# First scan of a Mamba-like layer: convolution on TensorE with diagonals, fewer rows spread by TensorE, and an earlier way out of the last chunk

## Chip, cores and metric

The kernel runs on one core of one Trainium2 chip. The metric is device time in microseconds (us) of one execution, lower is better. The kernel before takes 3999.52 us (median of three runs, 3998.8 to 4003.98).

## What is computed

The input x has 32 sequences of 256 tokens with 256 channels. A conditioned state-space layer runs first, then two layers of local attention with a gated feed-forward, and the result is added to x:

```
xr, gate = split(x @ W_in.T);  xr = xr + t_emb[:, None, :]
xc  = silu(conv over 4 tokens, one filter per channel (xr) + b_conv)
xn  = layernorm(xc)                       # 512 channels
Bm, Cm, dt = split(xn @ W_xproj.T)        # 16 states
Ad  = 1 + tanh(dt @ W_dt.T + b_dt) * 0.01 * A
Bd  = Bm * min(norm(xn), 1)
for t in range(256):
    h = clip(h * Ad[t] + Bd[t] * xn[t], -10, 10);  y[t] = Cm[t] . h
z = (y + D * xn) * silu(gate) @ W_out.T
z = two layers of (windowed attention, gated feed-forward)(z)
out = x + z
```

All arithmetic that matters here is in 32-bit floats.

## The kernel before

**Groups.** The 32 sequences are worked through in four groups of eight. One group's state (8 sequences x 16 states on 128 partitions, 512 channels on the free axis) is one tile h. The scan of a group has 256 steps; each is one custom VectorE instruction, `step` (L665), that adds a row to h and clips it. The steps are cut into 8 chunks of 32. The scan of group g + 1 is woven into the attention and feed-forward of group g. Only the first scan (`alone`, g == 0) has no such company; and the last group's attention has no scan beside it.

**A chunk.** `load_x` and `project` (L407) make the projection of x; `conv_in` (L437, L443) adds the conditioning to get xr and forms the first tap on GpSimd; `conv_taps` (L454) adds the other three taps on VectorE into acc; `conv_th` (L462, ScalarE) and `conv_out` (L467, VectorE) make the silu, xc. `raw_sums` (L476), `norm_turn` (L506), `norm_stats`, `norm_apply`, `norm_affine` (L540, L541 on GpSimd) and `norm_out` give the normalised rows and write them to DRAM as xnd. `length`, `figures`, `figures_out` (L570), `figures_in` and `decays` make the coefficients: beta that scales each row, ct for the read-out, and the clip bounds. All this runs some 40 steps ahead of the chunk that uses it.

**A step's row.** Row t must stand on all 16 states of its sequence. Either a DMA reads it from xnd with repetition (`load_rows`, L637, on the sync queue, six steps ahead, into one of seven xrep buffers), or, in the first scan only, TensorE spreads it (`spread_rows`, L645): a matmul with 32 rows of contraction, two at a time on different row groups, whose result bx lies in PSUM. `by_tensor` says which: t % 4 < 2, so half of the rows. ScalarE scales either kind by beta (`scale_row`, L658), and `step` consumes it.

**Out of a chunk.** `read_out` (L677) multiplies four h at a time with the diagonal ct (four matmuls with 32 output columns each, on different column groups) into y. `gated` (L726), `out_turn` (L732), `out_gate` (L746), `project_y` (L755), `copy_y` (L766) and `put_y` (L775) apply the skip and gate, project back to 256 channels and write ys to DRAM, from where `load_res` (L883) brings it for the attention, whose first work is `project_qkv` (L912).

**Order.** `group_scan` puts every piece on an agenda: `at(s, what, ...)` puts it at slot s, one slot for each step. `scan_to(s)` emits the slots up to s. The tile framework then orders the instructions of each engine by this order and by which are ready in its own plan; the engines work through their lists strictly in order. Buffers, PSUM banks (eight, all of one pool) and semaphore waits are allotted by the framework. The main part at the end loads layer 0's weights during the first scan, emits slots up to S + 18 (S = 256), loads the residual rows and starts the attention; from there the scan of the next group is emitted evenly with the attention's stages, up to slot 2 S + 18.

Of the kernel before, what the change touches and what calls it, by code (L numbers as in the profile page):

```python
# [10 lines left out]
FP = mybir.dt.float32  # L11
BF = mybir.dt.bfloat16
I32 = mybir.dt.int32
AF = mybir.ActivationFunctionType
ALU = mybir.AluOpType
# [4 lines left out]
P = 128  # L20
S = 256
DM = 256
KM = DM // P
DI = 512
NC_ = DI // P
NS = 16
GB = 8
CH = 32
NCH = S // CH
TB = P // GB  # L30
NQ = 4
# [3 lines left out]
XR = 2  # L35
TAPS = 4
# [16 lines left out]
def bc(ap, axis, n):  # L53

    ap = ap.unsqueeze(axis)
    shape = list(ap.shape)
    shape[axis] = n
    return ap.broadcast_to(shape)
# [15 lines left out]
def kernel(  # L74
# [29 lines left out]
    nc = tc.nc  # L104
# [33 lines left out]
    wc_sb = loaded(w_conv, [P, NC_, TAPS], "wc_sb")  # L138
    bconv_sb = loaded(b_conv, [P, NC_], "bconv_sb")
# [5 lines left out]
    ident = const.tile([P, P], FP, tag="ident", name="ident")  # L145
# [17 lines left out]
    for j in range(NJ):  # L163
# [18 lines left out]
        out=mask_t[:, 0:W], in_=mask_t[:, 0:W], compare_op=ALU.is_ge, fill=MASKED_LOW,  # L182
# [3 lines left out]
        out=mask_t[:, W : 2 * W], in_=mask_t[:, W : 2 * W], compare_op=ALU.is_ge,  # L186
# [29 lines left out]
    for i in range(2):  # L216
        t = const.tile([P, NI * (P + GB)], FP, tag=f"ly{i}", name=f"ly{i}")
# [3 lines left out]
    def program(ctx, exact):  # L221
        rpool = ctx.enter_context(tc.tile_pool(name="res", bufs=1, reuse_waits="tile"))
        wpool = ctx.enter_context(tc.tile_pool(name="weights", bufs=1, reuse_waits="tile"))
        sp = ctx.enter_context(tc.tile_pool(name="sp", bufs=1, reuse_waits="tile"))
# [6 lines left out]
        ps_w = ctx.enter_context(tc.tile_pool(name="psw", bufs=8, space=PSUM, reuse_waits="tile"))  # L231

        def bank(pool, tag, name):
            return pool.tile([P, DI], FP, tag=tag, name=name)
# [150 lines left out]
        def group_scan(g):  # L385
# [7 lines left out]
            b0 = g * GB  # L393
            alone = g == 0

            agendas = [{}]
            state = {"p": one}
            ck = [{} for _ in range(NCH)]

            def at(s, what, *args):  # L400
                agendas[-1].setdefault(s, []).append(partial(what, *args))
# [26 lines left out]
            def conv_in(c, ch):  # L428
                if ch == 0:
                    ck[c]["xc"] = sp.tile([P, NC_, GB * CH], FP, tag="xc", name="xc")  # L430
                ps = ck[c].pop(("ps", ch))
                xr = sp.tile([P, GB, TAPS - 1 + CH], FP, tag="xr", name="xr", bufs=2)
                if c == 0:
                    nc.gpsimd.memset(xr[:, :, 0 : TAPS - 1], 0.0)
                else:
                    nc.gpsimd.tensor_copy(xr[:, :, 0 : TAPS - 1], ck[c - 1]["carry"][:, ch])
                nc.vector.tensor_add(  # L437
                    xr[:, :, TAPS - 1 :],
                    ps.rearrange("p (b t) -> p b t", b=GB),
                    bc(cond_sb[:, ch, b0 : b0 + GB], 2, CH),  # L440
                )
                acc = sp.tile([P, GB, CH], FP, tag="acc", name="acc", bufs=2)
                nc.gpsimd.tensor_scalar(  # L443
                    acc, xr[:, :, 0:CH], wc_sb[:, ch, 0:1], bconv_sb[:, ch : ch + 1],
                    ALU.mult, ALU.add,
                )
                if c < NCH - 1:
                    nc.gpsimd.tensor_copy(ck[c]["carry"][:, ch], xr[:, :, CH:])
                ck[c]["xr", ch] = xr, acc

            def conv_taps(c, ch):
                xr, acc = ck[c]["xr", ch]
                for k in range(1, TAPS):
                    nc.vector.scalar_tensor_tensor(  # L454
                        acc, xr[:, :, k : k + CH], wc_sb[:, ch, k : k + 1], acc,
                        ALU.mult, ALU.add,
                    )

            def conv_th(c, ch):
                acc = ck[c]["xr", ch][1]  # L460
                th = sp.tile([P, GB * CH], FP, tag="th", name="th", bufs=2)
                nc.scalar.activation(th, acc.rearrange("p b t -> p (b t)"), AF.Tanh, scale=0.5)  # L462
                ck[c]["th", ch] = th

            def conv_out(c, ch):
                _, acc = ck[c].pop(("xr", ch))
                nc.vector.scalar_tensor_tensor(  # L467
                    ck[c]["xc"][:, ch], ck[c].pop(("th", ch)), 1.0,
                    acc.rearrange("p b t -> p (b t)"), ALU.add, ALU.mult,
                )  # L470


# [156 lines left out]
                return ck[c]["xnd"].rearrange("(b t) d -> b t d", b=GB)  # L629

            def by_tensor(t):
                return alone and t % NQ < XR

            def load_rows(c, t):
                xr = xp.tile([P, DI], FP, tag="xrep", name="xrep")
# [154 lines left out]
                )  # L790
                rep_w.append(t)

            rep_w = []
            at(-1, start)
            if alone:
                at(-30, spread_weights)
                constants(at)
            for c in range(NCH):
                for t in range(CH):
                    at(c * CH + t, step, c, t)  # L800
            for c in range(NCH):
                s0 = c * CH
                for hb in range(CH // TB):
                    s = s0 + hb * TB
                    for i in range(NI):
                        at(s + 4 * i + 5, read_out, c, hb, i)
                    at(s + 21, gated, c, hb)
                    at(s + 25, out_gate, c, hb)
                    at(s + 11, skip, c, hb)
                for ch in range(NC_):  # L810
                    at(s0 - 38 + 2 * ch, conv_in, c, ch)
                    at(s0 - 37 + 2 * ch, conv_taps, c, ch)
                    at(s0 - 36 + 2 * ch, conv_th, c, ch)
                    at(s0 - 35 + 2 * ch, conv_out, c, ch)
                for ch, s in enumerate((13, 16, 17, 18)):
                    at(s0 + s + 2, gate_th, c, ch)
                    at(s0 + s + 4, gate_out, c, ch)
                at(s0 - 25, raw_copy, c)
                at(s0 - 24, raw_turn, c)
                for j in range(NJ):  # L820
                    s = s0 - 26 + 4 * j
                    at(s + 2, norm_stats, c, j)
                    at(s + 4, norm_shift, c, j)
                    at(s + 5, norm_apply, c, j)
                    at(s + 6, norm_affine, c, j)
                    at(s + 9, norm_out, c, j)
                at(s0 - 11, length, c)
                at(s0 - 9, figures, c)
                at(s0 - 7, figures_in, c)
                at(s0 - 6, decay_th, c)  # L830
                at(s0 - 5, decays, c)
                at(s0 - 4, put_c, c, 0)
                at(s0 + 4, put_c, c, 1)
                for d in range(KM):
                    at(s0 + 45 + 2 * d, copy_y, c, d)
                    at(s0 + 46 + 2 * d, put_y, c, d)
            agendas.append({})
            for c in range(NCH):
                s0 = c * CH
                at(s0 - 43, load_x, c)  # L840
                for ch in range(NC_):
                    at(s0 - 40 + 2 * ch, project, c, ch)
                for ch, s in enumerate((13, 16, 17, 18)):
                    at(s0 + s, project, c, NC_ + ch)
                at(s0 - 27, raw_sums, c)
                for j in range(NJ):
                    at(s0 - 26 + 4 * j, norm_turn, c, j)
                at(s0 - 8, figures_out, c)
                for t in range(CH):
                    if not by_tensor(t):  # L850
                        at(s0 + t - 6, load_rows, c, t)
                    if by_tensor(t) and t % XR == 0:
                        at(s0 + t - 4, spread_rows, c, t)
                    at(s0 + t - 1, scale_row, c, t)
                for hb in range(CH // TB):
                    s = s0 + hb * TB
                    at(s - 9 if alone else s + 7, load_skip, c, hb)
                    at(s + 23, out_turn, c)
                for d in range(KM):
                    at(s0 + 43 + 2 * d, project_y, c, d)  # L860

            return agendas

# [40 lines left out]
        WEIGHTS = [("qkv", 2), ("qkv", 0), ("qkv", 1), ("wo", 0)]  # L904
# [67 lines left out]
        if exact:  # L972
# [4 lines left out]
                out=mask[:, 0:W], in_=mask[:, 0:W], compare_op=ALU.is_ge, fill=MASKED,  # L977
# [3 lines left out]
                out=mask[:, W : 2 * W], in_=mask[:, W : 2 * W], compare_op=ALU.is_ge, fill=MASKED,  # L981
# [402 lines left out]
        def scan_to(s):  # L1384
            while done[0] is None or done[0] < s:
                done[0] = next(scan, 1 << 30)


        DRAIN = 18
        for i, (kind, k) in enumerate(WEIGHTS):  # L1390
            scan_to(100 + 8 * i)
            load_weights(0, kind, k)
        scan_to(S + DRAIN)
        for b in range(GB):
            load_res(0, b)
        for w in range(NW):
# [4 lines left out]
        s0 = done[0]  # L1401
# [130 lines left out]
```

## Time and profile before

| what | value |
|---|---|
| median of three runs | 3999.52 us |
| profiled execution, its own time | 3989.48 us |
| its span | 3987.7 us |
| PE / DVE / ACT / POOL busy | 3769.4 / 2638.7 / 2321.3 / 1739.2 us |
| first step of the first scan | 52.8 us |
| first instruction of the second scan's state (start of h, L781) | 452.4 us |
| first qkv projection | 487.5 us |
| data moved by DMA | 353.51 MB, 89 GB/s on average |

PE is TensorE, DVE VectorE, ACT ScalarE, POOL GpSimd, SP the sync engine that issues most DMAs. The profile cuts the span into 40 slices and gives each engine's busy share in tenths; it lists groups of instructions by line and shape, and it answers with timelines of one engine, where neighbouring instructions of one line are merged and "x8" counts records. A 32-bit matmul leaves two records. An arrow ("<-") names what ended an idle time.

### The profile page before, as it was taken

How to read it: one execution, taken by the hardware profiler on the slowest of the kernel's cores; microseconds unless marked ns; L12 is line 12 of the kernel's file. 1: busy time of each engine (PE TensorE's matmuls, PEld its weight loads, DVE VectorE, ACT ScalarE, POOL GpSimd, SP SyncE). 2: the span in 40 equal slices, each digit the busy share in tenths (PEclk: the TensorE clock that was granted, in tenths of full speed). 3: DMA queues.
4: the chain of work that ended last, by engine and by line, in shares of the span. 5: the costliest groups of instructions: out<-in, count | busy, mean ns of one | idle time of the engine just before them, and what ended most of it. 6: DMA issues, size and time to landing. Idle time of an engine off the chain costs nothing.

```text
span 3987.7 us, 57891 instructions
## 1 busy us (share of the span) xinstructions
PE 3769.4 (95%) x20540; PEld 2359.2 (59%) x20540; DVE 2638.7 (66%) x5241; ACT 2321.3 (58%) x3893; POOL 1739.2 (44%) x1784
## 2 busy tenths in 40 slices
PE   7899889999999999999999999999999999999999
PEld 3333345666656666666666666566666666666666
DVE  6888887777766766767676677676677544444443
ACT  3555556666666566566666656556666555555553
POOL 4443364444444444544445444344444343433431
PEclk8999899999999999999999999999999999999999
DMA  5444533333433434233343434323333111000000
GB/s 152 116 119 118 159 111 110 89 107 103 106 98 97 124 109 128 84 93 94 91 112 94 118 106 116 101 83 101 94 101 103 36 36 44 1 17 20 18 14 23
DMA packets 360414, 353.51 MB, mean 89 GB/s; under 512 B 173795, under 2 KB 220212, under 8 KB 359988
## 3 DMA queue, kind: packets, MB, share of 16 engines
q1 hardware_dynamic: 275666, 337.71, 29.4%
q10 hardware_dynamic: 84450, 12.01, 1.9%
q8 instruction: 165, 2.70, 0.3%
q14 instruction: 133, 1.09, 0.1%
HBM read 314.49 MB, written 33.55 MB: 87 GB/s over the span
## 4 chain that ended last, share of the span: by engine, by line
PE 44%; DVE 16%; ACT 13%; DMA 11%; POOL 9%; issue 5%; ACTq 1%; SPq 0%; DVEq 0%; POOLq 0%
DMA xrep<-xnd 10%; PE ps_qkv L912 9%; PE pa L1247 8%; PE po_f L1275 5%; DVE h L665 5%; PE y L677 3%; ACT xrep L658 3%; PE ps_wo L962 3%; PE sc L1118 3%; PE ov L1156 2%; POOL rn L944 2%; ACT L1255 2%; DVE acc L454 2%; PE ps_in L407 2%; ACT L1127 2%
## 5 line engine op out<-in xcount | busy, mean ns | idle before, releaser
L658 ACT ACTIVATE xrep<-xrep,beta 128x512 f32<-128x512 f32 x896 | 631.1, 722 | 692.2 <-DMA xrep<-xnd 532.4
L665 DVE CUSTOM_DVE_ANT_0 h<-h,xrep,lim 128x512 f32<-128x512 f32 x1024 | 918.6, 897 | 52.7 <-PE y L677 12.5
L912 PE MATMUL ps_qkv<-qkv,res 128*128 128x512 f32 x1536 | 718.0, 604 | 34.6 <-ACT qT L956 21.7
L1247 PE MATMUL pa<-hT,w 128*128 128x256 f32 (+1 forms) x3072 | 693.0, 388 | 28.0 <-ACT pT L1127 26.8
L936 POOL TENSOR_TENSOR rot<-rot,swp 128x512 f32<-128x512 f32 x256 | 344.1, 1344 | 766.3 <-DVE swp L933 621.5
L1247 PEld LDWEIGHTS pa<-hT,w 128*128 128x128 f32 (+1 forms) x3072 | 502.4, 179 | 192.1 <-issue 63.3
L1263 DVE SCALAR_TENSOR_TENSOR ag<-pa,b_sb,ag 128x256 f32<-128x256 f32 (+1 forms) x448 | 213.1, 476 | 594.6 <-ACT ag L1255 593.2
L912 PEld LDWEIGHTS ps_qkv<-qkv,res 128*128 128x128 f32 x1536 | 279.2, 192 | 314.6 <-issue 247.4
L944 POOL TENSOR_TENSOR rn<-ss,neg_half 128x8 f32<-128x8 f32 x256 | 444.2, 1735 | 11.5 <-DVE ss L942 1.6
L1275 PE MATMUL po_f<-ag,w 128*128 128x256 f32 (+1 forms) x1536 | 385.4, 392 | 17.9 <-DVE res L1286 9.3
L677 PE MATMUL y<-h,ly 128*32 128x512 f32 x2048 | 369.1, 620 | 20.1 <-DVE h L665 19.5
L1275 PEld LDWEIGHTS po_f<-ag,w 128*128 128x128 f32 (+1 forms) x1536 | 273.9, 189 | 124.3 <-issue 44.4
L407 PE MATMUL ps_in<-xg,w_in_sb 128*128 128x256 f32 x1024 | 285.9, 410 | 18.0 <-DMA xg<-in_xT_dram 10.4
L945 POOL TENSOR_TENSOR rot<-rot,rn 128x512 f32<-128x512 f32 x256 | 287.7, 1124 | 20.0
L1206 POOL TENSOR_TENSOR rstd<-ve,neg_half 128x1 f32<-128x1 f32 x128 | 77.0, 602 | 486.6 <-DVE ve L1204 486.6
L407 PEld LDWEIGHTS ps_in<-xg,w_in_sb 128*128 128x128 f32 x1024 | 190.8, 199 | 145.7 <-issue 62.0
L928 DVE TENSOR_TENSOR rot<-ps_qkv,rc_sb 128x512 f32<-128x512 f32 x256 | 175.6, 686 | 139.0 <-ACT sq L925 137.8
L1127 ACT ACTIVATE pT<-sc 128x512 f32<-128x512 f32 x384 | 208.3, 594 | 94.9 <-PE sc L1118 93.3
L454 DVE SCALAR_TENSOR_TENSOR acc<-xr,wc_sb,acc 128x256 f32<-128x256 f32 x384 | 203.4, 532 | 89.2 <-POOL acc L443 88.1
L1127 ACT ACT_TABLE_LOAD x185 | 237.4, 1283 | 24.5 <-PE sc L1118 21.5
L1255 ACT ACTIVATE ag<-pa,b_sb 128x256 f32<-128x256 f32 x320 | 151.7, 474 | 156.8 <-PE pa L1247 152.4
L1255 ACT ACT_TABLE_LOAD x186 | 238.6, 1283 | 3.3
(149 smaller groups left out, 5765.7 us busy)
## 6 DMA issues: line engine op xcount, KB each, us to landing
xrep<-xnd SPq DMA_DIRECT2D x896, 256.0 KB
xnd<-xn SPq DMA_DIRECT2D x64, 256.0 KB
qkv<-in_wqkv_dram SPq DMA_DIRECT2D x24, 512.0 KB
xd<-xnd SPq DMA_DIRECT2D x192, 64.0 KB
w<-in_w_dram SPq DMA_DIRECT2D x80, 128.0 KB
xg<-in_xT_dram SPq DMA_DIRECT2D x64, 128.0 KB
ys<-yo ACTq DMA_DIRECT2D x64, 128.0 KB
res<-ys SPq DMA_DIRECT2D x32, 256.0 KB
```

Of the source, the lines that this page charges most:

```text
L407: nc.tensor.matmul(ps, w_in_sb[:, k, ch * P : (ch + 1) * P], ck[c]["xg"][:, k], start=(k == 0), stop=(k == KM - 1),)
L658: nc.scalar.activation(bx, ck[c].pop(("bx", t), bx), AF.Copy, scale=ck[c]["beta"][:, t : t + 1])
L665: nc.vector._custom_dve(TENSOR_ADD_SAT, out=h_new, in0=state["h"], in1=bx, s0=ck[c]["lim"][:, 0, t : t + 1], s1=ck[c]["lim"][:, 1, t : t + 1],
L677: nc.tensor.matmul(ck[c]["y", hb][32 * q : 32 * q + 32, :], ly[hb % 2][:, 32 * t : 32 * t + 32], ck[c].pop(("h", hb * TB + t)), start=(i = ...
L912: nc.tensor.matmul(ps, res[b][:, k, t0 : t0 + W], wt["qkv", a][:, k], start=(k == 0), stop=(k == KM - 1),)
L936: nc.gpsimd.tensor_add(rot, rot, swp)
L944: nc.gpsimd.tensor_tensor(rn, ss, neg_half, ALU.pow)
L945: nc.gpsimd.tensor_mul(rot, rot, bc(rn, 2, DH))
L1127: nc.scalar.activation(p, banks[r], AF.Exp)
L1247: nc.tensor.matmul(pg if x else pa, wt["w1", m][:, k, x], self.h[:, k], start=(k == 0), stop=(k == KM - 1),)
L1255: nc.scalar.activation(ag[0:n], pg, AF.Gelu, bias=b1g)
L1275: nc.tensor.matmul(self.po[:, d], wt["w2", 0][r0 : r0 + n, m, d * P : (d + 1) * P], self.ag[m][r0 : r0 + n], start=(m == 0), stop=(m == le ...
```

## The change

In the first scan only:

- **Convolution.** The four taps become matmuls on TensorE: each multiplies xr, shifted by k tokens, with a 128 x 128 diagonal matrix of the channel's tap weights, and a matmul with a contraction of one row adds the bias. They accumulate in PSUM, where ScalarE and VectorE read them. The first tap on GpSimd and the three on VectorE go. The sixteen diagonals (four taps for each of four blocks of channels), the bias row and a row of ones are made once, in the buffers that later hold the qkv weights.
- **Rows.** `by_tensor` becomes t % 8 < 2: a quarter of the rows are spread by TensorE, three quarters come by DMA.
- **Weights.** wo, w1 and w2 are asked for first, from slot 64 on; qkv at slot 226, since its buffers hold the diagonals until the last convolution.
- **Last chunk.** The second half of the first scan's last chunk has its gate, transpose, output projection, copy and store at earlier slots, and the main part goes on at S + 7 in place of S + 18.

```diff
+            def end(c, hb):
+                return alone and c == NCH - 1 and hb == CH // TB - 1
...
             def conv_taps(c, ch):
...
+                    acc = bank(ps_w, "w", "ps_conv")[:, 0 : GB * CH]
+                    nc.tensor.matmul(
+                        acc,
+                        tap_w[2][0:1, 0, ch * P : (ch + 1) * P],
+                        tap_w[2][0:1, 1, 0 : GB * CH],
+                        start=True,
+                        stop=False,
+                    )
+                    for k in range(TAPS):
+                        nc.tensor.matmul(
+                            acc.rearrange("p (b t) -> p b t", b=GB),
+                            tap_w[ch // KM][:, ch % KM, k * P : (k + 1) * P],
+                            xr[:, :, k : k + CH],
+                            start=False,
+                            stop=(k == TAPS - 1),
+                        )
...
             def by_tensor(t):
-                return alone and t % NQ < XR
+                return alone and t % (2 * NQ) < XR
...
+            def tap_weights(i):
+                t = wpool.tile([P, KM, DI], FP, tag=f"qkv{i}", name="tap_w")
+                nc.vector.tensor_mul(
+                    t.rearrange("p c (k n) -> p c k n", k=TAPS),
+                    bc(bc(ident, 1, TAPS), 1, KM),
+                    bc(wc_sb[:, i * KM : (i + 1) * KM], 3, P),
+                )
+                tap_w.append(t)
+
+            def tap_bias():
+                t = wpool.tile([P, KM, DI], FP, tag="qkv2", name="tap_b")
+                nc.scalar.dma_start(
+                    out=t[0:1, 0].rearrange("p (c n) -> p c n", c=NC_),
+                    in_=b_conv.rearrange("p c -> c p").unsqueeze(0),
+                )
+                nc.gpsimd.memset(t[0:1, 1], 1.0)
+                tap_w.append(t)
...
+                for i in range(NC_ // KM):
+                    at(-41, tap_weights, i)
+                at(-41, tap_bias)
...
-                    at(s + 21, gated, c, hb)
-                    at(s + 25, out_gate, c, hb)
+                    at(s + (21, 18)[end(c, hb)], gated, c, hb)
+                    at(s + (25, 19)[end(c, hb)], out_gate, c, hb)
...
-                    at(s0 + 45 + 2 * d, copy_y, c, d)
-                    at(s0 + 46 + 2 * d, put_y, c, d)
+                    at(s0 + (45 + 2 * d, 37 + d)[end(c, 1)], copy_y, c, d)
+                    at(s0 + (46 + 2 * d, 37 + d)[end(c, 1)], put_y, c, d)
...
-                    at(s + 23, out_turn, c)
+                    at(s + (23, 18)[end(c, hb)], out_turn, c)
...
-                    at(s0 + 43 + 2 * d, project_y, c, d)
+                    at(s0 + (43 + 2 * d, 36)[end(c, 1)], project_y, c, d)
...
-        for i, (kind, k) in enumerate(WEIGHTS):
-            scan_to(100 + 8 * i)
+        for i, (kind, k) in enumerate(WEIGHTS[3:] + WEIGHTS[:3]):
+            scan_to(S - 30 if kind == "qkv" else S // 4 + 8 * i)
             load_weights(0, kind, k)
-        scan_to(S + DRAIN)
+        scan_to(S + 7)
```

`bc` broadcasts an operand along a new axis; `bank` takes one PSUM bank.

## The prediction

> **What bounds the kernel now.** I read the forty slices first, then busy time by stage, then the costliest groups and the timelines of TensorE (PE) and VectorE (DVE) in one chunk of the first scan, and last the way out of that scan.
>
> ```profile
> PE   7899889999999999999999999999999999999999
> DVE  6888887777766766767676677676677544444443
> ```
>
> From the sixth slice on PE is at its ceiling and DVE is not. The first five slices (500 us) are the first scan, which no attention accompanies. A kernel that is PE-bound afterwards gains only by ending this scan sooner without leaving PE work for later. The steps of the first scan run from 52.8 to 451.9 us: 399 us for 8 chunks of 32 steps. A table of busy time for a steady chunk (us, PE, weight loads, DVE, ACT, POOL, clock, DMA share, GB/s):
>
> ```profile
> 299.50:349.00 49.50, 45.14 (x172) 17.97 (x169) 45.07 (x83) 29.59 (x55) 19.88 (x26) 0.93 0.42 119
> ```
>
> Both PE and DVE are busy 91% of it, so neither can be the bound alone: each waits for the other in its fixed order. Groups of instructions by shape, 100 to 400 us (about 6 chunks; busy us, mean ns, idle before):
>
> ```profile
> L677 PE MATMUL y<-h,ly 128*32 128x512 f32 x384 | 107.5, 657 | 7.1 <-DVE h L665 6.6
> L645 PE MATMUL bx<-xq,rep_w 32*128 32x512 f32 x194 | 61.1, 638 | 0.0
> L407 PE MATMUL ps_in<-xg,w_in_sb 128*128 128x256 f32 x192 | 57.3, 437 | 0.0
> ...
> L454 DVE SCALAR_TENSOR_TENSOR acc<-xr,wc_sb,acc 128x256 f32<-128x256 f32 x73 | 36.8, 504 | 5.6 <-POOL acc L443 5.6
> ```
>
> A matmul leaves two records here (L407 issues 16 a chunk, and 192 records stand for 6 chunks). How long does one take? The PE timeline says it (start, length, line, count of records):
>
> ```profile
> 250.03 1.07 PE L677 MATMUL y<-h,ly 128*32 128x512 f32 x8
> 251.02 1.13 PE L407 MATMUL ps_in<-xg,w_in_sb 128*128 128x256 f32 x4
> 252.08 1.13 PE L645 MATMUL bx<-xq,rep_w 32*128 32x512 f32 x4
> ...
> 255.53 1.04 PE L677 MATMUL y<-h,ly 128*32 128x512 f32 x2
> ```
>
> From start to start: two full 256-column matmuls 1.06, so 0.53 each; a pair of bx 1.06; four y in a row 1.0, but one y alone also 0.98. And DVE, beside the convolution:
>
> ```profile
> 305.10 0.48 DVE L454 SCALAR_TENSOR_TENSOR acc<-xr,wc_sb,acc 128x256 f32<-128x256 f32 x1 [0.46 <-POOL acc L443]
> 305.50 0.81 DVE L665 CUSTOM_DVE_ANT_0 h<-h,xrep,lim 128x512 f32<-128x512 f32 x1
> 306.23 0.63 DVE L454 SCALAR_TENSOR_TENSOR acc<-xr,wc_sb,acc 128x256 f32<-128x256 f32 x1
> ```
>
> A tap takes 0.40 of DVE from start to start, waits for POOL's first term now and then, and is slower (0.63) while POOL works. The way out, from the last output projection to the first qkv:
>
> ```profile
> 472.77 0.70 PE L755 MATMUL ps_out<-zT,w_out_sb 128*128 128x256 f32 x2
> ...
> 487.48 8.35 PE L912 MATMUL ps_qkv<-qkv,res 128*128 128x512 f32 x12 [6.54 <-ACT xrep L658]
> ```
>
> From the last step at 451.9 to qkv at 487.5 are 35.6 us; the named releaser had long been done, the data came through ys and the res loads (issued from 482.5).
>
> **What the Trainium skill says.** "TensorE: Matmul & The Clock Gate", Part 3 on packing small matmuls: a small contraction or output saves nothing by itself, only neighbours on other row or column groups overlap. The trace agrees: one y 0.98, four 1.0. "Trainium Kernel Development and Optimization", Performance Expectations: matmul busy time is a poor measure of nearness to the limit. Here it holds for y: 18 us busy per chunk (17.36 in the chunk above, mean 18.4), where eight runs of four would need 8. "SBUF — State Buffer", Who interferes with whom: a DVE operation with two SBUF inputs and a POOL operation that reads SBUF exclude each other. The trace agrees in kind: POOL's first term takes 0.56 alone and 1.28 beside DVE. "DMA: Bandwidth & Descriptors", Queues, rings and completion order: descriptors of one issuing engine's ring are consumed in order. No row of before shows a large load in the middle of the first scan.
>
> **The change, part by part.** The order in which the changed program issues its instructions shows that it does what it says: 32 convolutions of 5 matmuls, 64 bx in place of 128, 192 row loads in place of 128, and no L454 in the first scan.
>
> *DVE per chunk.* Out: 12 taps x 0.40 = 4.8, waits for POOL's first term 5.6/6 = 0.9, slowing beside POOL 4 x 0.2 = 0.8. Back: taps filled the gap between dependent steps (0.88 from step to step back to back, 0.72 with something between); the new order has 11 such pairs a chunk, the old 8: 3 x 0.16 = 0.5. Net -6.0 to -6.4. xc now reads PSUM; other DVE rows that read PSUM (L437, 415 ns; L746, 667) are no slower than SBUF ones, so nothing. ACT's th likewise (its PSUM row is 677, its SBUF row 721).
>
> *PE per chunk.* In: 4 x 5 x 0.53 = 10.6, the one-row bias priced as a full matmul (bounds 0 to 0.53; nothing on other row groups is next to it). Out: 4 bx pairs, and the split pairs: nine runs become four, 5 x 1.06 = 5.3. y: the old order has 12 runs a chunk (up to 18 in the first), the new one 8, and the single y that wait for single steps are gone. Sum for a new steady chunk: y 8.0, bx 4.2, ps_in 8.5, conv 10.6, ps_out 3.9, ps_raw 2.0, transposes 3.1, ps_st 1.0 = 41.3. The same sum for the old one is 40 against 45 busy and 49.5 elapsed.
>
> *The new wait.* On PE the convolution waits for xr, which DVE writes (L437), and behind it stand the next ps_in and a run of y. Who waits for those: DVE's next xr, and the h buffers. In the new order each xr stands at least one step ahead of its convolution, so I price no wait beyond the stretches below. PSUM has eight banks; a chunk takes 34 of them in turn now and 30 after the change (8 bx fewer, 4 convolutions more), so none is short.
>
> *Together.* PE and DVE meet every four steps, when a run of y needs its fourth h. In the new order the eight PE stretches are about 6.8, 7.4, 4.7, 4.2, 4.7, 5.1, 4.2, 3.7 us (two convolutions fall into the second, ps_in and bx into the first). Those of DVE, with steps at 0.74 to 0.88 and the waits for POOL's powers (10.3/6 = 1.7) that stay, are 4.9, 4.8, 4.3, 4.1, 4.7, 6.1, 5.5, 6.5. The later of each pair sums to 45.9. Eight h buffers let DVE run ahead of PE in the first two: I take 1 off, 45.0. Bounds: 43 (DVE alone, 49.5 - 6.4) to 48. Gain 4.5 a chunk. The convolutions of chunks 1 to 7 fall into the first seven; chunk 7 carries that of the next group, on DVE as before, and no gain. 7 x 4.5 = 31.5.
>
> *Row loads.* 24 of 32 rows now come by DMA: 8 x 262 KB more, 5.9 to 8.0 MB a chunk, 176 GB/s at 45 us. Between 455 and 487 us, with every row loaded, 24 steps took 33 us (1.4 each) at 191 GB/s. So the rate is there, and I price it at nothing; cover is the seven row buffers. Without it ACT waits for 2 to 4 us more a chunk, as it does now behind xnd. SP issues 8 more at 0.52, 4 us, beside waits of its own.
>
> *Ramp.* The two tap tables (128x1024 products, by L726's 680 ns for 512 about 1.4 each) and the small bias load fall into DVE's 3.8 us idle and before x lands at 10.4. The four convolutions then take PE 10.6 in the ramp, where DVE needed 12 taps; POOL's chain (L289, L540, L541) ends last. 0, bounds -3 to +3.
>
> *Weights.* wo, w1, w2 move ahead, qkv behind: 1.5 MB now stand on SP's queue after row 150 of 192, with row loads behind them. At 260 GB/s, which full windows show, they need 6 us; row buffers hold some 4. Once +2, bounds 0 to 6.
>
> *Way out.* Its last transposes, zT and ps_out now stand directly after the last y, and nothing but 14 steps of the next group stands ahead of qkv. Old steps 1 to 14 of that group end 21 us after the scan; the path y, transpose, ps_out (about 8) plus the old 14.7 from ps_out to qkv gives 23. So 35.6 becomes 23: -12.6. PE work shifted behind it: eight ps_in 4.2, two y, small ones: +5.6. Net -7, bounds -12 to -2. Eleven slots less in the drain mean the second scan's remaining steps are spread 4% denser over a PE-bound stretch; their PE work is the 5.6 already counted.
>
> *Sum.* -31.5 - 7 + 2 = -36.5. The profiled execution took 3989.5 (span 3987.7), so 3953; the median of the runs is 10 higher, 3999.5, so 3963.
>
> **Rivals.** *DVE was the whole bound:* each chunk loses 6.4 and the way out 12.6: 45 + 13 = 58, 3942. For it: DVE's waits on PE inside a chunk are small (h idle 5.4 in 300 us). Against: PE's 7 us stretches. *PE hands the gain back in part:* its 41.3 with all its old idle (4.4) and some 2 of remaining waits, 48 a chunk: 10.5 + 7 - 2 = 15.5, 3984. *Slower:* in the convolution's stretch the y do not close up, because h still arrive singly, each waiting for a row. Then y stay at 18.4 and PE's busy time is 45.1 - 5.3 + 10.6 = 50.4, with 4.4 idle 54.8: +5.3 x 7 = 37, less 5, 4032. It decides from y above about 14 us a chunk. Against it: the order itself writes them in fours.
>
> **Numbers.** Forecast 3963 (3950 to 3977) 55%; DVE the whole bound, 3942, 12%; partly handed back, 3984, 15%; slower, 4032, 15%; anything else 3%. About 0.2%, 8 us, is what a measurement of this kernel can tell from no change. Faster 78%, within it 8% (upper end of the third case, lower of the fourth), slower 14%. The range 3940 to 3988 takes in the first three.
>
> **What would show it.** Right: chunks of about 45 us, PE near 42 busy with y at 9 to 11, DVE near 39; no L443 or L454 before the second scan; qkv some 23 us after the last step. Wrong: y still 15 or more a chunk, ACT's waits for row loads grown past 4 us a chunk, or a gap of over 6 us where qkv is loaded.

## The result, and the profile after

The kernel before took 4003.87 us (median of 13 runs beside those of the changed kernel), the changed one 3990.97 (3981.46 to 3996.99): a ratio of 0.9968 with a 95% interval of 0.9959 to 0.9976, 13 us less where 37 were forecast. The profiled execution of the kernel before was a lucky one, 14 us under that median, and that of the changed kernel 6 under its own; so the two spans, 3987.7 and 3983.4, differ by only 4. Totals below are therefore ratios, each against runs of the kernel before on the same chip; stages are read from the traces.

The slices of the changed kernel, PE and DVE:

```profile
PE   7888789989999999999999999999999999999999
DVE  5878777677777766767676677676667544444443
```

DVE has become lighter in three of the first five slices (the first scan), and PE is no fuller there. Busy time of a steady chunk of the changed kernel (start:end, length, PE, weight loads, DVE, ACT, POOL, clock, DMA share, GB/s):

```profile
196.14:244.07 47.93, 42.19 (x198) 22.60 (x196) 37.42 (x69) 29.36 (x56) 17.06 (x29) 0.96 0.62 167
```

The chunk lost 1.6 us of 49.5, though DVE lost 7.6 of busy time and PE 3. Both now stand idle for longer. Groups of the changed kernel, 100 to 400 us:

```profile
L703 PE MATMUL y<-h,ly 128*32 128x512 f32 x402 | 77.1, 630 | 4.5 <-DVE h L691 4.4
L471 PE MATMUL ps_conv<-xr,tap_w 128*128 128x256 f32 x177 | 44.3, 390 | 0.0
L671 PE MATMUL bx<-xq,rep_w 32*128 32x512 f32 x100 | 31.4, 634 | 0.0
...
L463 PE MATMUL ps_conv<-tap_b 1*128 1x256 f32 x44 | 15.3, 426 | 0.0
```
```profile
L493 DVE SCALAR_TENSOR_TENSOR xc<-th,ps_conv 128x256 f32<-128x256 f32 x23 | 9.7, 421 | 21.4 <-ACT th L489 21.2
...
L552 DVE SCALAR_TENSOR_TENSOR stat<-mv,stat 128x1 f32<-128x1 f32 x12 | 3.0, 250 | 17.9 <-POOL stat L547 17.5
```

```profile
L596 PE MATMUL ps_st<-rhs,sel 128*128 128x96 f32 x24 | 6.6, 417 | 24.3 <-ACT xrep L684 20.5 <-DVE rhs L588 3.8
```

The same three places in the kernel before:

```profile
L467 DVE SCALAR_TENSOR_TENSOR xc<-th,acc 128x256 f32<-128x256 f32 x24 | 11.5, 479 | 4.8 <-ACT th L462 4.8
L526 DVE SCALAR_TENSOR_TENSOR stat<-mv,stat 128x1 f32<-128x1 f32 x12 | 7.2, 598 | 10.3 <-POOL stat L521 10.3
L570 PE MATMUL ps_st<-rhs,sel 128*128 128x96 f32 x24 | 6.3, 402 | 17.5 <-DVE rhs L562 14.6 <-ACT xrep L658 2.9
```

On PE, y fell from 107.5 to 77.1 and bx from 61.1 to 31.4; the convolution came in with 59.6. On DVE the waits for ACT's th (now L493) and for the power on POOL (now L552) rose from 4.8 and 10.3 us to 21.4 and 17.9; PE's wait at ps_st, the product of the figures, rose from 17.5 to 24.3. In one chunk they look like this; first DVE, then POOL, then PE:

```profile
219.67 0.17 DVE L552 SCALAR_TENSOR_TENSOR stat<-mv,stat 128x1 f32<-128x1 f32 x1 [4.26 <-POOL stat L547]
219.79 0.81 DVE L691 CUSTOM_DVE_ANT_0 h<-h,xrep,lim 128x512 f32<-128x512 f32 x1
```
```profile
217.86 1.27 POOL L567 TENSOR_TENSOR xn<-xn,lnb_sb 128x512 f32<-128x512 f32 x1
219.09 0.55 POOL L547 TENSOR_TENSOR stat<-ve,neg_half 128x1 f32<-128x1 f32 x1
```
```profile
232.78 1.14 PE L596 MATMUL ps_st<-rhs,sel 128*128 128x96 f32 x4 [4.21 <-ACT xrep L684]
```

DVE stands 4.26 us at a tiny operation, with steps of h queued behind it. What it waits for is a power on POOL (L547, the inverse root of a variance), and POOL does that only after its passes over xn of the chunk's first half (L566, L567). Some thirteen microseconds on, PE stands 4.21 us at the product of the figures, with the next chunk's ps_in and a run of y behind it. (In the kernel before the second wait was 2.9, the first 1.7.)

The way out, on PE:

```profile
448.11 5.16 PE L781 MATMUL ps_out<-zT,w_out_sb 128*128 128x256 f32 x16 [1.10 <-DVE zT L772]
...
463.08 3.24 PE L961 MATMUL ps_qkv<-qkv,res 128*128 128x512 f32 x7 [0.64 <-DMA res<-ys]
```

From the last step (ends 439.7) to qkv are 23.4 us, as forecast, and qkv starts 24.4 us earlier than before. But from there to the end it takes 3520.3 us in place of 3500.2. Most of the head start is given back. (The profiled execution before was fast for its kernel, so these 20 us are too many rather than too few.)

### The profile page after: what moved, and what is told of

The parts are those of the page before. It is cut to its first block, busy times and chain, and to the rows that moved or that the text cites. A ratio compares the mean times of both kernels' runs of the same rounds, so it can differ in the third digit from the quotient of the medians.

```text
span 3983.4 us, 58306 instructions
## 1 busy us (share of the span) xinstructions
PE 3756.7 (94%) x20732; PEld 2400.9 (60%) x20732; DVE 2586.4 (65%) x5147; ACT 2325.8 (58%) x3893; POOL 1715.3 (43%) x1753
## 4 chain that ended last, share of the span: by engine, by line
PE 44%; DVE 15%; ACT 14%; DMA 11%; POOL 10%; issue 5%; ACTq 1%; SPq 0%; DVEq 0%; POOLq 0%
DMA xrep<-xnd 10%; PE ps_qkv L961 9%; PE pa L1296 8%; PE po_f L1324 5%; DVE h L691 4%; ACT xrep L684 4%; POOL rn L993 3%; PE ps_wo L1011 3%; PE y L703 2%; PE ov L1205 2%; PE sc L1167 2%; ACT L1304 2%; PE ps_in L412 2%; POOL rot L985 2%; DVE acc L480 2%
## 5 line engine op out<-in xcount | busy, mean ns | idle before, releaser
L684 ACT ACTIVATE xrep<-xrep,beta 128x512 f32<-128x512 f32 x960 | 677.2, 722 | 721.9 <-DMA xrep<-xnd 508.8
L691 DVE CUSTOM_DVE_ANT_0 h<-h,xrep,lim 128x512 f32<-128x512 f32 x1024 | 912.6, 891 | 65.8 <-PE y L703 17.9
L703 PE MATMUL y<-h,ly 128*32 128x512 f32 x2048 | 322.7, 617 | 14.5 <-DVE h L691 14.4
L1011 PE MATMUL ps_wo<-oT,wo 128*128 128x256 f32 x1024 | 231.5, 379 | 0.0
```

The lines of the kernel that those rows point to most:

```text
L684: nc.scalar.activation(bx, ck[c].pop(("bx", t), bx), AF.Copy, scale=ck[c]["beta"][:, t : t + 1])
L691: nc.vector._custom_dve(TENSOR_ADD_SAT, out=h_new, in0=state["h"], in1=bx, s0=ck[c]["lim"][:, 0, t : t + 1], s1=ck[c]["lim"][:, 1, t : t + 1],
L703: nc.tensor.matmul(ck[c]["y", hb][32 * q : 32 * q + 32, :], ly[hb % 2][:, 32 * t : 32 * t + 32], ck[c].pop(("h", hb * TB + t)), start=(i = ...
L1011: nc.tensor.matmul(po[:, d], wt["wo", 0][:, c, d * P : (d + 1) * P], oT[:, c, :], start=(c == 0), stop=(c == NC_ - 1),)
```

## The experiments

"Chunk" is the mean interval of 32 steps over chunks 1 to 5, read from the starts of the h steps in each trace; "behind" is the time from the first qkv to the end. Chunk, qkv and behind come from one trace each. The change, e3 and e11 have the same loop and agree in the chunk to 0.1 us, but their first steps come between 53.5 and 58.1 us, so a few microseconds in the last two columns mean nothing. Each expectation says what it means by its theories.

| kernel | ratio to before (95%) | chunk, us | qkv at, us | behind, us |
|---|---|---|---|---|
| before | 1 | 49.7 | 487.5 | 3500.2 |
| the change | 0.9968 (0.9959 to 0.9976) | 48.1 | 463.1 | 3520.3 |
| e3 convolution and rows | 0.9942 (0.9928 to 0.9955) | 48.2 | 479.5 | 3495.3 |
| e1 convolution alone | 0.9995 (0.9983 to 1.0006) | 50.6 | 491.8 | 3494.7 |
| e2 rows alone | 0.9977 (0.9969 to 0.9985) | 48.7 | 482.5 | 3504.6 |
| e4 way out alone | 1.0016 (1.0009 to 1.0022) | 49.5 | 477.0 | 3525.6 |
| e7 change, half the rows | 1.0031 (1.0020 to 1.0043) | 51.1 | 486.1 | 3522.4 |
| e6 change, no bias | 0.9950 (0.9936 to 0.9964) | 47.8 | 457.1 | 3517.1 |
| e10 e3, figures later | 0.9967 (0.9955 to 0.9979) | 48.4 | 489.8 | 3489.9 |
| e14 e3, one power | 1.0030 (1.0019 to 1.0041) | 49.0 | 480.7 | 3521.2 |
| e16 e10, xg by POOL | 1.0014 (1.0005 to 1.0024) | 47.5 | 497.4 | 3497.1 |
| e17 e3, xn by DVE | 0.9898 (0.9884 to 0.9912) | 43.6 | 454.7 | 3500.8 |
| e18 e16 and e17 | 0.9947 (0.9934 to 0.9959) | 46.3 | 483.5 | 3493.7 |
| e21 before, xn by DVE | 0.9967 (0.9956 to 0.9978) | 46.9 | 468.6 | 3502.4 |
| e25 e3, third pass on POOL | 0.9984 (0.9976 to 0.9992) | 49.0 | 488.8 | 3497.8 |
| e26 before, third pass | 1.0035 (1.0025 to 1.0045) | 50.7 | 502.6 | 3500.2 |
| e11 change, scan first | 0.9947 (0.9935 to 0.9959) | 48.2 | 473.5 | 3501.9 |
| e22 change, xn by DVE | 0.9904 (0.9885 to 0.9923) | 43.1 | 437.4 | 3521.3 |

**The parts.** e3 leaves out the short way out, e4 puts it alone on the kernel before (the same slots, and `scan_to(S + 7)`); e1 and e7 keep half the rows on TensorE, e2 changes the rows alone. e3, e1 and e7 keep the changed order of the weights.

```diff
 e3, e1:
-                return alone and c == NCH - 1 and hb == CH // TB - 1
+                return False
-        scan_to(S + 7)
+        scan_to(S + DRAIN)
 e1, e7 (e2 the other way round, on the kernel before):
-                return alone and t % (2 * NQ) < XR
+                return alone and t % NQ < XR
```

> The change without the shorter way out (slots of the last chunk and S + 18 as before); convolution by TensorE, quarter of the rows, order of the weights as changed. Theory P (in the first scan TensorE's own list sets the chunk: 42 us of work and 5.5 us of waits in its order): chunks stay near 47.7 us, the first scan still ends near 440 us, qkv starts some 12 us later than in the changed kernel (475), and from qkv to the end it takes 10 to 15 us less than there (3505 to 3510), because work that the early start pushed behind it is done before; total 3991 to 3997. Rival (the prediction's sum: an earlier start is worth 7 us net): total 7 us above the changed kernel, 3998.

> The kernel before with the shorter way out alone. Theory P with the early start given back: qkv starts 10 to 14 us earlier than before (475), from there to the end it takes nearly as much longer (3508 to 3514 where before took 3500); total within 4 us of before, 4000 to 4004. Rival (the prediction's sum): 7 us less than before, 3997.

> The changed kernel with half of the rows spread by TensorE again. Theory P: four more pairs of bx, 4.2 us more TensorE work a chunk, chunks near 52 us, the first scan some 30 us longer, total 4015 to 4022, slower than before. Rival D (rows that come late by DMA hold the chunk at 47.7): with 8 loads fewer a chunk gets shorter, 45 to 47, total 3975 to 3990. Rival W (VectorE's waits in its own list): chunks unchanged, total 3991.

> The kernel before with one edit: a quarter of the rows spread by TensorE, convolution still on VectorE, way out as before. PE loses some 4.2 us of bx a chunk, VectorE loses nothing. If the gain of the change comes from VectorE's lighter list (theory V), the chunk stays at 49 to 49.5 us and the time at 0.999 to 1.001 of the kernel before. If the gain comes from fewer spread rows alone, and the convolution by TensorE gives nothing or takes back (theory R; the change with half the rows was 1.003), the chunk falls to 46.5 to 47.7 and the ratio to 0.992 to 0.996.

> The change's convolution by TensorE alone: half the rows still spread by TensorE, way out as before. With the short way out this was 1.0031; that way out costs 0.0016 to 0.0026. So 1.0005 to 1.0015 if the parts add. The rows alone gave 0.9977, both together 0.9942: then the two edits are worth more together than their sum (0.998 to 0.999). If it is under 0.998, they simply add and the half rows in the run with the short way out lost elsewhere.

The loop's two edits together gain 0.58%, 23 us (18 to 29). Neither does so alone: the convolution nothing (its chunk is 1 us longer, and the chunk beside the load of qkv takes 56.3), the rows 0.23%. A reading that fits is that PE, busy 46 of 51 us in e1, has no room for 10.2 us of convolution until bx gives some back. e7 bears it out: four more pairs of bx, 4.2 us, made the change's chunk 3.0 us longer. The way out costs 0.16% alone; with the rest it takes 0.26 points off e3's gain. That is the first half of the answer: without its third part the change is faster. Only e7 came out as its theory said; e3 was better and e4 dearer than either of their theories, e1 and e2 lay between theirs.

By its first qkv e3 is only 8 us ahead of the kernel before (479.5 against 487.5), and its steady chunk gains 1.5 us. The other 15 of its 23 us lie behind. Part of that is the fast profiled execution before, which was not fast in the first scan: e4, with the same first scan, ends it at 451.5 us against 452.3. The rest wasn't looked into.

**Is PE's work the bound of the chunk?** e6 leaves out the bias matmul, and so the addition of b_conv: four matmuls of 0.62 us a chunk.

```diff
-                    nc.tensor.matmul(acc, tap_w[2][0:1, 0, ...], tap_w[2][0:1, 1, ...],
-                        start=True, stop=False)
-                            start=False,
+                            start=(k == 0),
```

> The changed kernel without the bias matmul (it leaves out the convolution's bias, and starts the sum with the first tap). Theory P: 4 x 0.62 = 2.5 us less TensorE work a chunk, chunks near 45.3 us, total 14 to 18 us less than the changed kernel, 3973 to 3977. Rivals D and W: chunks unchanged, total within 3 us of 3991.

The first chunk fell to 43.7 us (47.4), steady ones stayed at 47.6 to 48.0. But e6 does not decide. PE's run from ps_st to the transposes is as long as with the bias, 24.4 us, with the same number of y and ps_in in it: they take about 1.4 and 0.8 us longer. In e6's list one of the runs of four y is split into three and one, and what stands behind PE's wait is slowed for longer (1.94 us for four y; the change has 1.40 there):

```profile
181.65 1.94 PE L696 MATMUL y<-h,ly 128*32 128x512 f32 x8
185.28 1.06 PE L696 MATMUL y<-h,ly 128*32 128x512 f32 x6
190.31 1.04 PE L696 MATMUL y<-h,ly 128*32 128x512 f32 x2
```

So PE was spared little, 1.0 us of busy time a chunk, and the chunk fell by 0.4; the total, 7 us under the change, lies between the theories. The chain of e3, in order of time (start, length), suggests another bound, which e17 and e26 below test:

```profile
211.33 0.59 PE tp_x L532 x4
...
219.11 1.28 POOL xn L566
...
220.47 1.27 POOL xn L567
221.73 0.52 POOL stat L547
...
222.28 0.18 DVE stat L552
...
231.54 0.72 ACT sq_x L573 x2
...
235.38 0.71 PE ps_st L596 x2
```

It is a ring. PE works without a stop from ps_st at 187.4 through the next chunk's ps_in and convolutions to the transposes of the norm at 212; then 23 us of latency lead over POOL, DVE, eight steps of h held up at L552, and ACT back to ps_st at 235.4: 25 + 23 = 48. (From sq_x the data of ps_st go over DVE's ss at 232.4, a second power on POOL at 232.7, 1.2 us long, and rhs on DVE at 233.9; the view follows ACT's list, which runs beside them.)

**Where can the ring be shortened?** e10 puts figures_out, figures_in, decay_th, decays and put_c one slot later; e14 does both halves' power in one instruction, with the steps that use it behind; e16 is e10 with xg loaded through GpSimd's list; e17 gives the two passes over xn to VectorE in the first scan; e18 is e16 and e17; e21 is e17's edit on the kernel before. The edits of e10, e14 and e16 hold in all four scans, those of xn in the first alone.

```diff
 e10:
-                at(s0 - 8, figures_out, c)
+                at(s0 - 7, figures_out, c)
 e14:
-                nc.gpsimd.tensor_tensor(stat[:, j, 0:1], ve, neg_half[:, 0:1], ALU.pow)
+                if j == NJ - 1:
+                    nc.gpsimd.tensor_tensor(stat[:, :, 0], ve, neg_half[:, 0:NJ], ALU.pow)
 e16:
-                    nc.sync.dma_start(out=xg[:, k], ...)
+                    nc.gpsimd.dma_start(out=xg[:, k], ...)
 e17, e21:
+                eng = nc.vector if alone else nc.gpsimd
-                nc.gpsimd.tensor_mul(xn, xn, lng_sb)
-                nc.gpsimd.tensor_add(xn, xn, lnb_sb)
+                eng.tensor_mul(xn, xn, lng_sb)
+                eng.tensor_add(xn, xn, lnb_sb)
```

> The change with the long way out (0.9942 of the kernel before), and in it the product of the figures (ps_st on PE) with what follows it (figures_in to put_c) one step later. In the trace of the change PE stands 4.2 us a chunk at ps_st, behind it the y runs, the next chunk's ps_in and its convolution. If that wait sets the chunk (theory L, a chain through lists kept in order), the chunk falls by 2 to 4 us and the ratio to 0.987 to 0.990. If the wait only takes up slack (the chunk is set by VectorE's stall at stat or by the chain of h), the chunk stays at 47 to 48 and the ratio at 0.993 to 0.996; if the later figures make h wait, it is 0.996 or more.

> The change with the long way out (0.9942), and in it one power on GpSimd for both halves of the chunk, with both norm_shifts, norm_applys and xn passes after it, so that the power of half 1 no longer stands behind the two xn passes of half 0. VectorE waits 4.3 us a chunk there (stat behind POOL), with steps of h behind it. If this stall sets the chunk (theory S), the wait goes, the chunk falls by 2 to 4 us and the ratio to 0.987 to 0.990. If the chain over PE's wait at ps_st sets it (theory L), the stall moves: the last xn pass comes no earlier, since both now follow half 1, the wait at ps_st stays at 4 us or grows, and the ratio stays at 0.993 to 0.997.

> The change with the long way out, the product of the figures one step later (alone that gave 0.9967: PE's wait of 4 us went from ps_st to the next chunk's ps_in, which waited for xg behind the writes of xn and the loads of xq in SP's list), and xg loaded through GpSimd's list in place of SP's. Theory R (ring): PE's next run starts when xg is there, and no more at 191.4 us but at 185 to 187 us in the same chunk's time, 1 to 5 us a chunk less than the 48.3 of the figures alone: 44 to 47, ratio 0.987 to 0.993. Theory V: PE's wait goes, or moves to the y runs, and the chunk stays at 47.5 to 48.5, ratio 0.994 to 0.998.

> The two edits of the runs beside it together: figures one step later with xg through GpSimd's list, and xn by VectorE in the first scan. Theory R (ring): both waits leave the ring, so the gains add until VectorE's work (37.5 + 2.5 us) or PE's (42) sets the chunk: 42 to 45, ratio 0.980 to 0.989. Theory V: 47.5 to 50, ratio 0.994 to 1.000.

> The change with the long way out (0.9942 of the kernel before; chunks 47 to 48 us), and in the first scan the two passes over xn (norm_affine) by VectorE in place of GpSimd, so that the power of half 1 has no pass ahead of it on GpSimd and each pass takes less time (1.28 us on GpSimd). Theory R (ring): the steady chunk is a ring of 24.5 us in which PE works through its list from ps_st to the transposes of the norm without a stop, and 23.5 us of latency from these transposes over stat, xn, power, stat, eight steps of h, sq_x, rhs back to ps_st. This edit takes 2.5 to 5 us out of the latency and adds some 2.5 us of work to VectorE, which has 8 to 10 us of slack: chunk 43.5 to 46, ratio 0.984 to 0.991. Theory V (VectorE's work and the chain of h set the chunk, the stalls only take up slack): the chunk stays at 47.5 or grows by up to 2.5 us, ratio 0.994 to 0.999.

> The kernel before (convolution by VectorE) with the one edit that in the first scan VectorE does the two passes over xn in place of GpSimd. In the kernel before VectorE was busy 44 to 45 of 49.4 us. If VectorE's work set the chunk there (the ring is what the change made the bound), 2.5 us more of it cost 1 to 3 us a chunk: ratio 1.001 to 1.005. If the ring over the norm set the chunk there already, it gains as it does with the change: ratio 0.990 to 0.997.

e10 missed: PE's wait went from ps_st to the next ps_in and was about as long (3.5 to 4.1). The PE timeline of e10:

```profile
191.44 2.04 PE L412 MATMUL ps_in<-xg,w_in_sb 128*128 128x256 f32 x4 [3.50 <-DMA xg<-in_xT_dram]
```

The loads of xg stand in SP's list behind the loads of xq, which wait for the written xn; so xg closes the same ring a second time. e16 takes it out of that list, and PE still waits 2.3 to 3.1 us a chunk at ps_in: xg through GpSimd lands late. The view of that tile in e16:

```profile
DMA to landing us min/median/max: 5.8/6.7/7.8
```

(through SP the chain of e10 shows 3.6.) e18 keeps that wait, 2.3 to 4.7, and is worse than e17 alone. e16's steady chunk, 47.5, is even shorter than e3's; it loses at the start (first step at 64.6 us against 56.3, first chunk 53.8 against 47.5). e14 moves the stall from L552 to the steps of h (3.0 to 3.4 us a chunk, e3 1.5 to 1.9), and 26 us of its loss against e3 lie behind the first scan (3521.2 against 3495.3), where the same norm runs beside attention: a wait exchanged for a wait. e14 and e16 came out worse than either of their theories. e17 is the hit, 43.6 us a chunk. Two groups of e17, 100 to 400 us:

```profile
L567 DVE TENSOR_TENSOR xn<-xn,lng_sb 128x512 f32<-128x512 f32 x12 | 8.2, 685 | 1.5 <-ACT xn L559 1.5
...
L552 DVE SCALAR_TENSOR_TENSOR stat<-mv,stat 128x1 f32<-128x1 f32 x14 | 3.8, 273 | 5.4 <-POOL stat L547 5.0
```

A pass takes 0.69 us in place of 1.27, as the Trainium skill has it ("GPSIMD Engine Reference", Engine selection: an elementwise operation with two inputs is about twice as slow on GpSimd). The power no longer queues, and the wait at L552 falls from 19.7 us (e3) to 5.4. PE's wait at ps_st falls from 4.2 to 0.3 in chunks 2 and 3. DVE got 2.7 us more work a chunk and the chunk became 4.7 us shorter. PE's busy time fell by only 0.8 us (42.4 to 41.6), so it was not PE's sum that set the chunk. The same edit gained 2.8 us a chunk in the kernel before.

The edit did more than shorten the latency, though. Here are the steps of h, e3 and then e17:

```profile
L691 DVE CUSTOM_DVE_ANT_0 h<-h,xrep,lim 128x512 f32<-128x512 f32 x196 | 169.6, 865 | 12.6 <-ACT xrep L684 4.7 <-DVE h L691 2.9 <-PE ps_raw L502 0.8
L692 DVE CUSTOM_DVE_ANT_0 h<-h,xrep,lim 128x512 f32<-128x512 f32 x214 | 178.6, 835 | 9.6 <-ACT xrep L685 2.6 <-PE y L704 1.9 <-DVE h L692 1.0
```

With less work on POOL beside it a step takes 0.03 us less, 1 us a chunk; DVE's busy time rose by 0.9 us and not by 2.7, and in e21 it fell, from 44.6 to 43.4. And PE, without its long wait, kept a higher clock, 0.98 over these chunks in place of 0.94 (last section).

Was it the latency, or only less crowding on GpSimd? e25 (on e3) and e26 (on the kernel before) add a pass on GpSimd, and no work to PE or VectorE:

```diff
                 nc.gpsimd.tensor_add(xn, xn, lnb_sb)
+                if alone:
+                    nc.gpsimd.tensor_scalar_mul(xn, xn, 1.0)
```

> The change with the long way out (0.9942), and in the first scan a third pass over each half of xn on GpSimd, a multiplication by 1.0, behind the power of half 1. It adds 1 to 2.5 us of latency a chunk between the norm and the product of the figures, and no work to PE or VectorE; GpSimd is idle 30 us of 48. Theory R (the chunk is a ring through this latency): the chunk grows by 1 to 2.5 us, ratio 0.996 to 0.999. Theory T (moving xn to VectorE helped only by ending the contention of GpSimd's passes with VectorE's, or by the earlier power): 0 to 0.5 us, ratio 0.993 to 0.9955.

> The kernel before with the same third pass on GpSimd in the first scan. Moving xn to VectorE gained 0.9967 there too. If the ring bound the kernel before as well, the chunk grows by 1 to 2.5 us, ratio 1.002 to 1.0045; if it was bound by VectorE's work with the power of half 1 in it, 0 to 0.5 us, ratio 0.9995 to 1.0015.

The pass takes 1.7 us a half and stands behind the power, on an engine that is idle for 30 us of the chunk; 17 us were lost in one kernel and 14 in the other (0.42 and 0.35%). Part of the loss lies in the chunks (0.7 and 1.0 us each, where 1 to 2.5 were expected), part in the start of the scan (in e26 the first chunk takes 59.4 us, before 53.3). In e26 DVE's busy time did not grow (44.6 and 44.3 us a chunk), so there it is latency that made the chunk longer: the ring was in the bound of the kernel before, which the prediction did not have. In e25 DVE's busy time grew by 1.0 us as well, so there latency and crowding are not told apart. How much of e17's 4.7 us is latency, crowding or clock was not separated.

**The way out.** e11 keeps the short way out and the early loads of res, but does the scan's list up to its old point before the first projections.

```diff
             load_res(0, b)
+        scan_to(S + DRAIN)
         for w in range(NW):
```

> The whole change, short way out included, but the last steps of the scan's list (S + 7 to S + 18, which hold early work of the second scan) are put before the first projections of the first sequence and not beside them; only the loads of res stay early. The change itself was 0.9968, with the long way out 0.9942. Theory G (the early start of attention only brings forward work that then shares PE with what the second scan's start needs, and the later sequences give it back): qkv begins near 473 us in place of 463, the part after it falls from 3520 to 3495 to 3500, and the ratio is 0.992 to 0.9945. If instead the shortened steps of the last chunk themselves (gated, out_turn and project_y moved up) cause the loss, the part after stays at 3515 or more and the ratio is 0.996 to 1.0.

> The whole change, short way out and all, with the two passes over xn by VectorE in the first scan. With the long way out this edit gave 0.9898. If the price of the short way out (0.9968 against 0.9942) is paid behind the first scan and has nothing to do with its chunks (theory G), it is paid again: 0.9915 to 0.993, and the second scan's first 32 steps take 88 to 92 us in place of 79. If the price came from the chunks being late, it goes: 0.988 to 0.990.

e11 starts qkv 10 us later than the change, "behind" falls from 3520 to 3502, and the total by 0.21 points, 8 us. So the moved steps of the last chunk are innocent of most of it; the cost is that projections start before the second scan has its early work done. The total, 0.9947, is just above what this theory said (0.992 to 0.9945). In the changed kernel, on DVE:

```profile
483.28 4.40 DVE L691 CUSTOM_DVE_ANT_0 h<-h,xrep,lim 128x512 f32<-128x512 f32 x4
495.06 0.69 DVE L977 TENSOR_TENSOR rot<-ps_qkv,rc_sb 128x512 f32<-128x512 f32 x1 [7.37 <-ACT sq L974]
```

VectorE waits 7.4 us for squares of the projections, and the steps of the second scan stand behind: from its step 14 to 24 it takes 45.7 us (before 24.2), for its first 32 steps 90.6 (before 80.8, e11 75.2, e4 90.9, e22 89.6). PE, which is the bound there, starves a little later. Busy time of 520 to 600 us, first the change, then e11:

```profile
520.00:600.00 80.00, 66.46 (x372) 38.40 (x369) 61.52 (x115) 44.32 (x83) 42.03 (x43) 0.94 0.42 113
```
```profile
520.00:600.00 80.00, 72.54 (x427) 40.11 (x425) 68.13 (x129) 46.78 (x88) 44.88 (x48) 0.98 0.47 129
```

The trace of e22 speaks against a link with the chunks: with them at 43.1 us qkv starts at 437.4, and "behind" is 3521.3 again. Its total does not show it: 0.9904 can't be told from e17's 0.9898, while the price seen between e3 and the change would make it 0.9924, which is just outside its interval (to 0.9923). Which wait accounts for which part of the 20 us was not separated; what PE loses in the first eight sequences, both layers, is 13.7 us of idle and 9.1 of busy time, some of it at a lower clock.

## Why the prediction was wrong

*The direction held, the size did not:* 13 us came of 36.5 in the sum, and 3991 lies above the range. Two steps failed: "Together", which made the loop 6.5 us worse than forecast by the totals, and "Way out", 17 us. None of the three signs named for being wrong appeared; they watched for other failures. Term by term:

- *DVE per chunk, -6.0 to -6.4:* right or a little low; busy 45.1 to 37.4 in the chunks shown.
- *PE's sum, 41.3:* 42.2 busy, right in part by luck. y takes 12.3 us a chunk where 8.0 was summed and 9 to 11 named as the sign of success: single y were not gone. The other terms came out lower (a convolution 2.55 us, four taps 1.93 and the bias 0.62, against 2.65 priced; the transposes 2.5 against 3.1), and the busy time counts overlaps once. The slower rival (y stays at 18) fell.
- *"Together", the later of each pair of stretches, 45.9, less 1:* this step failed. It let PE and DVE wait for each other alone. The waits for POOL's powers "that stay" at 1.7 became 2.9; the waits of xc for ACT's th went from 0.8 to 3.4; and "no wait beyond the stretches" on PE left out ps_st, 4.2 us. All three are places of one ring through PE, ACT, POOL and DVE, whose latency DVE's lighter list hardly shortens: 48.1 us a chunk where 45.0 was forecast, a gain of 1.6 in place of 4.5. By the totals the loop gained 23 us (e3) where 31.5 less 2 was forecast. The counter-test: with the ring cut short on both sides (e17 against e21) convolution and rows gain 0.69%, 27.5 us (about 20 to 35), near the 29.5; their chunks differ by 3.3 us. That speaks for the prices, with a latency that was not priced taking part of them; it does not prove each.
- *Row loads, 0:* right. ACT's waits for rows were 67.0 us in 300 before and 58.9 after.
- *Ramp, 0:* right as far as one trace tells; the first step comes at 53.5 us in place of 52.8, but at 56.3 and 58.1 in e3 and e11.
- *Weights, +2 (0 to 6):* the two chunks beside the load of qkv take 49.7 and 51.1 us, 5.4 over the steady 47.7 together: at the upper end. In e3 they are 8 over.
- *Way out, 35.6 to 23, net -7:* this step failed too, and by more. The 23 was exact (23.4; the old last step ends at 452.3 and not 451.9, so 35.2 before), the net wrong in sign, because only PE work moved behind qkv was charged (+5.6). e4 measured +6.4 us, and 10 between e3 and the change. What failed is the sentence that the denser steps cost nothing more: e11, with the same early loads and these steps ahead of the projections, got 8 us back, so their order against the projections' in the engines' lists does cost.

The rival that came nearest, 3984 with 48 us a chunk, had the size of the chunk by another account: PE's work with its old idle time and some waits. e17 shows that these waits could be taken out with PE's work nearly as it was. And it had the way out at -7, so its nearness to 3991 is luck.

## What to carry to other kernels

Where two engines are both about 90% busy and neither is full, follow the chain of waits once around a whole period before adding up either's work: a chunk can be a ring of latency, and then work taken off an engine turns into a wait on it. Look first at small operations that stand behind large ones on a slow engine; moving 2.7 us of work to a busier but faster engine gave more (0.44%) than the change's net gain (0.32%). Starting the next phase early pays only if its instructions are not put, in the lists of shared engines, ahead of what the phase that is PE-bound will need.

## What was not expected of the hardware

In the trace of the change a bias, a matmul over a single row, takes 0.62 us for 256 columns from start to start, where a tap over 128 rows takes 0.48.

The clock that TensorE is granted falls after its waits. In the changed kernel, behind the wait of 4.21 us that ends at 232.78 (a window, then four records of ps_in inside and four outside it):

```profile
232.70:236.00 3.30, 3.22 (x12) 2.23 (x16) 3.30 (x7) 1.38 (x3) 0.00 (x0) 0.50 0.68 187
```
```profile
233.71 1.97 PE L412 MATMUL ps_in<-xg,w_in_sb 128*128 128x256 f32 x4
236.79 1.13 PE L412 MATMUL ps_in<-xg,w_in_sb 128*128 128x256 f32 x4
```

The clock is 0.50, and four records take 1.97 us in place of 1.13. Two successive chunks of e17:

```profile
148.92:194.80 45.88, 42.38 (x192) 22.49 (x192) 39.29 (x73) 29.87 (x56) 13.64 (x18) 0.89 0.65 173
194.80:236.10 41.30, 40.70 (x198) 21.77 (x197) 38.27 (x73) 28.33 (x54) 13.53 (x25) 1.00 0.70 190
```

The first has one gap of 3.09 us on PE (at ps_out, behind zT) and the clock at 0.89; the second has none over 0.31, and 1.00. The Trainium skill ("TensorE: Matmul & The Clock Gate", Part 1) has the clock fall to half after an idle window of about 3.4 us. The half agrees; the length does not. Here 3.09 us was enough, and so was the 2.89 at ps_st in the kernel before:

```profile
193.20:196.40 3.20, 3.20 (x13) 1.12 (x12) 3.06 (x6) 1.05 (x2) 0.00 (x0) 0.50 0.65 190
```

A wait of 2.08 us at 424.4 in the changed kernel was not followed by it (clock 1.00 from 424.3 to 429.0). The depth of the loss does not go with the length of the gap: the chunk of the changed kernel, with its 4.21, had 0.96 on average. So in these traces a wait of some three microseconds on PE cost more than its length. How much of a chunk this is worth stays open: e3 and e11 with 0.94 over their steady chunks and the change with 0.95 have the same 48.2.
